# Cross attention's keys and values by Strassen's method, in a fused decoder and gated cross-attention kernel

## The chip, the cores and the metric

The kernel runs on one core of one Trainium2 chip, in float32 throughout. The metric is the device time of one execution in microseconds (us); less is better. A core has five engines with an instruction queue each: PE (matrix products), DVE, ACT and POOL (elementwise work), and SP, which here does nothing but issue DMAs. Each works through its own queue in order and waits at an instruction until what it needs is there.

## The reference

Sixteen sequences of 128 tokens with 512 channels and 16 heads of 32 go through a decoder layer (self-attention, cross-attention to `ctx_2048`, MLP) and then a gated cross-attention to the normalized `ctx_2048`. Cut to what matters here:

```python
ln_out = layernorm(hidden_states, ln1_s, ln1_b)
q, k, v = jnp.split(ln_out @ w_qkv + b_qkv, 3, axis=-1)
x = hidden_states + merge_heads(attention(q, k, v, ltor_mask)) @ w_ao + b_ao     # per head
ln_out = layernorm(x, ln2_s, ln2_b)
q = ln_out @ w_q + b_q
k, v = jnp.split(encoder_states @ w_kv + b_kv, 2, axis=-1)
x = x + merge_heads(attention(q, k, v, cross_mask)) @ w_co + b_co
x = x + gelu(layernorm(x, ln3_s, ln3_b) @ w1 + b1) @ w2 + b2
# then: x + tanh(gate) * gated cross attention of x to layernorm(encoder_states)
```

The change concerns the line with `w_kv`, the keys and values of cross-attention.

## The kernel before

**Groups, batches, units, steps.** The 16 sequences are four groups of four batches. A group's activations `x[g]` stay in SBUF from start to end (128 partitions, 4 batches, 512 channels). An attention stage is a list of sections, one for each group: A0 to A3 (self-attention), B0 to B3 (cross-attention), D0 to D3 (gated). `attend` goes through a section in 16 steps, four for each batch; a step handles one unit, four heads of one batch. In the step k of unit k, PE makes the scores (at each batch's first step), DVE scales them and POOL adds the mask; one step later DVE takes the minimum and ACT the exponentials (four activations); two steps later DVE takes the reciprocal of the sums and POOL normalizes; three steps later DVE transposes in 32x32 squares and SP sends the tile to device memory (`away`). The pair of units comes back as `pT` five steps later, PE mixes the values at step 10 counted from the batch's first (`mix`, product `av`), ACT copies the result (`mT`), and PE makes the output projection (`mo`) at step 12, which DVE adds to `x[g]`.

**Work beside the attention.** Beside section n stand the jobs of section n+1 (`jobs`: its queries, keys and values) and the preparations of section n+2 (`prepare`: normalizing `x[g]`, sending it to device memory and back so that channels lie on the partitions, loading the encoder's rows in blocks). So group 0's cross-attention projections run beside A3, and those of groups 1 to 3 beside B0, B1 and B2. Which job stands in which step is written out by hand: `plan` takes lists of jobs with lists of steps, and the order of the program is the order of every queue. `afterwards` defers an instruction to the start of the next step (`due`).

**Plain and Strassen projections.** A plain projection (`project_chunk`, `values_chunk`) makes 4 chunks of 4 matmuls with 512 columns. `block_product` makes the same as a product of 2x2 blocks by Strassen's method in Winograd's form: 7 products of 4 matmuls with 256 columns. `left_blocks` and `right_blocks` give the blocks and the four sums on either side. Products 1, 6 and 7 add up in one PSUM bank (`mm0`), which ACT copies out after each; 5 and 3 share `mm1`; 2 and 4 take `pt`, and DVE adds these in. Before the change self-attention and gated attention make queries, keys and values so; cross-attention makes all three plainly, with the value bias as a row (`bcv`) that DVE adds to the values. Tables such as `SECOND_BLOCKS` and `BLOCKS` say which product stands in which step:

```python
    SECOND_BLOCKS = (
        {4: (1, 2), 5: (6, 5), 6: (7, 4), 8: (3,)},
        {7: (1, 2), 8: (6,), 9: (7, 5), 10: (4,), 11: (3,)},
        {12: (1,), 13: (6, 2), 14: (7, 5), 15: (4, 3)},
    )
```

**Other work in these stages.** The weights of the gated stage are loaded as blocks, turned by DVE and written back to device memory (`gated_weight`): k and v beside self-attention, q beside B0 and o beside B1, with the loads in steps 0 to 7 and the turns in steps 8, 10, 12 and 14. Beside B2, `FirstGated.prepare` loads the turned k and v weights. Beside B3 run the first gated keys and values (`beside_last_cross`) and the first pieces of the MLP. Weight tiles rotate through six buffers (tag `w`), score tiles through eight (tag `s`), which the MLP and the last batch's transposes use too. Nearly all instructions are issued through a helper on line 49, so rows of the profile all name L49 and are told apart by their tiles: `mm_k_B` is the PSUM tile of cross-attention's keys, `mm_v_B` that of its values, `mo_B` and `mT_B` as above; `_A` is self-attention, `_D` gated attention, `h` and `o` the MLP.

Of the kernel before, what the change touches and what calls it, by code (L numbers as in the profile page):

```python
# [16 lines left out]
P = 128  # L17
NB = 16
S = 128
Q = 32  # L20
# [32 lines left out]
def decoder_then_gated_cross_attention(ctx: ExitStack, tc: tile.TileContext, a: dict, out: bass.AP):  # L53
# [24 lines left out]
    def afterwards(engine, do):  # L78
        late[engine].append(do)
# [32 lines left out]
    for b in range(GB):  # L112
# [8 lines left out]
            ("b_k", a["L0_xattn_b_kv"][0:H]), ("ln3_s", a["L0_xattn_ln3_s"]), ("ln3_b", a["L0_xattn_ln3_b"]),  # L121
# [199 lines left out]
    def values_chunk(v, wt, actT, b, name, bias_row=None):  # L321
# [4 lines left out]
        if bias_row is None:  # L326
            afterwards("act", lambda: nc.scalar.copy(v[:, b, :], mm))
        else:
            afterwards("dve", lambda: nc.vector.tensor_tensor(v[:, b, :], mm, bias_row, ALU.add))
# [151 lines left out]

    GATED_BLOCKS = (
# [54 lines left out]
    def scale_unit(bt, j):  # L537
        s = work.tile([P, NQ, KC, Q], F32, tag="s", name=f"s_{bt.name}_{j}", bufs=8)
        if bt.by_array:
            s = s.rearrange("p n c j -> p (n c j)").rearrange("p (c n j) -> p n c j", c=KC, n=NQ)  # L540
        bt.s[j] = s
        bt.sec.scale_mask(by_head(s), bt.sc.pop(j).rearrange("p (c n k) -> p c n k", c=KC, n=NQ), bt.b)
# [30 lines left out]
    def turn_by_array(bt, j):  # L573

        s = by_head(bt.s.pop(j)).rearrange("p c n k -> p c (n k)")
        tp = ps("sc", f"tp_{bt.name}_{j}")
        for c in range(KC):
            nc.tensor.transpose(tp[:, c * S : (c + 1) * S], s[:, c], ident)
        pT = work.tile([P, KC, NQ, Q], F32, tag="s", name=f"pT_{bt.name}_{j}", bufs=8)
# [263 lines left out]

    CROSS = {
# [15 lines left out]
    class CrossAttention(Section):  # L860
# [123 lines left out]
    def mlp(ml, last_steps):  # L984
# [8 lines left out]
        def sums_of(g, t):  # L993
            s3, s2, s4 = (quarter(work, "s", f"sx{n}_{g}", 8) for n in range(3))
# [103 lines left out]
        def projected_out(g, p, mm, acc):  # L1098
# [3 lines left out]
            if p == 0:  # L1102
                acc["m1"] = quarter(work, "s", f"m1_{g}", 8)
# [6 lines left out]
            elif p == 5:  # L1110
                acc["u2"] = quarter(work, "s", f"u2_{g}", 8)
                add(acc["u2"], mm, acc["m1"], ALU.add)
                gadd(x12, x12, acc["u2"], ALU.add)
            elif p == 6:
                acc["u3"] = quarter(work, "s", f"u3_{g}", 8)
# [3 lines left out]
            elif p == 4:  # L1119
                m5 = quarter(work, "s", f"m5_{g}", 8)  # L1120
# [97 lines left out]
    def fetch_part(key, t, n):  # L1218
        nc.sync.dma_start(out=t[:, n], in_=gated[key][:, n])
# [26 lines left out]

    class FirstGated:


        def prepare(self, p):  # L1250
# [5 lines left out]
            elif p < 3 * GB:  # L1256
                key, k = ("gk", "gv")[p // GB - 1], p % GB
# [246 lines left out]
    def beside_last_cross():  # L1504
        flip[0] = 2
        def piece():
# [6 lines left out]
            *gated_start(first), *mlp_start(ml), ([piece] * len(at_), at_),  # L1513
# [93 lines left out]
```

## Time and profile before

| | |
|---|---|
| Median of 3 runs | 1185.05 us (1183.89 to 1185.69) |
| The profiled execution | 1185.11 us, span 1183.2 us |
| PE busy | 1148.6 us (97%), 7010 records |
| DVE busy | 754.2 us (64%) |
| ACT busy | 592.6 us (50%) |
| POOL busy | 673.9 us (57%) |
| DMA | 253.70 MB, mean 214 GB/s |
| Mean granted PE clock | 0.992 |

The span is the time from the first to the last instruction; what lies around it is the difference to the execution's time. A busy share is an average over stages with different limits, so what bounds a stage is read from that stage alone. Every float32 matmul leaves two records in the trace, so counts of PE records are twice those of instructions. In rows of engines, the number after "x" is the count; "mean ns" is the mean duration of one; what stands in brackets with an arrow is what ended the idle time ahead of the instruction.

### The profile page before, as it was taken

The page shows a single profiled execution, that of the slowest core. Times are in us where ns is not written, and L with a number is a line of the kernel's source. Part 1 is how long each engine was busy: PE and PEld are TensorE (multiplying, and loading weights), DVE is VectorE, ACT ScalarE, POOL GpSimd, SP SyncE. Part 2 cuts the span into 40 slices and gives each one's busy share as a digit, 9 for nine tenths or more (in the row PEclk, how much of TensorE's full clock was granted, in tenths as well). Part 3 has the DMA queues.
Part 4 walks back from the last instruction along what each step waited for, and adds up shares of the span by engine and source line. Part 5 has one row for each costly group of instructions (what it writes and reads, how often), then busy time and mean ns, then how long its engine had stood idle before and what let it go on. Part 6 is the DMA issues. An engine that isn't in the chain of part 4 may idle for free.

```text
span 1183.2 us, 21051 instructions
## 1 busy us (share of the span) xinstructions
PE 1148.6 (97%) x7010; PEld 828.7 (70%) x7010; DVE 754.2 (64%) x1493; ACT 592.6 (50%) x2061; POOL 673.9 (57%) x612
## 2 busy tenths in 40 slices
PE   6999999999999999998999999999999989999998
PEld 5877777644444444445788888888888767778775
DVE  7677878776877767867644534442432268887773
ACT  2467767666655656655321223222222237876753
POOL 6698878675757656676233514433341356554873
PEclk9999999999999999998999999999999999999999
DMA  6588979898988978798796484596457728988874
GB/s 215 145 216 225 234 191 221 227 266 199 200 229 196 238 211 226 195 276 254 237 309 219 135 270 167 182 294 224 152 177 257 202 56 219 233 226 240 247 205 161
DMA packets 321796, 253.70 MB, mean 214 GB/s; under 512 B 83156, under 2 KB 279960, under 8 KB 316824
## 3 DMA queue, kind: packets, MB, share of 16 engines
q1 hardware_dynamic: 321648, 252.34, 75.5%
q8 instruction: 56, 0.92, 0.3%
q14 instruction: 52, 0.43, 0.1%
q10 hardware_dynamic: 40, 0.01, 0.0%
HBM read 161.06 MB, written 91.23 MB: 213 GB/s over the span
## 4 chain that ended last, share of the span: by engine, by line
PE 50%; DVE 1%; ACT 1%; issue 1%; POOL 1%; DMA 0%; SPq 0%; POOLq 0%; ACTq 0%
PE h L49 16%; PE o L49 16%; PE mm_q_D L49 4%; PE mm_v_D L49 3%; PE mm_k_D L49 3%; PE mm_o_D L49 3%; PE sc_D L49 1%; PE av_D L49 1%; PE mo_D L49 1%; PE mo_B L49 1%; POOL x L49 1%; ACT s_B L49 0%; DVE s_D L49 0%; DMA pT_D<-away_D 0%; ACT v_D L49 0%
## 5 line engine op out<-in xcount | busy, mean ns | idle before, releaser
L49 ACT ACTIVATE s_B<-s_B,mn_B 128x128 f32<-128x128 f32 x256 | 99.5, 391 | 74.3 <-issue 54.4
L49 DVE TENSOR_TENSOR h<-h,h 128x512 f32<-128x512 f32 x80 | 54.9, 686 | 117.3 <-PE h L49 117.0
L49 ACT ACTIVATE s_A<-s_A,mn_A 128x128 f32<-128x128 f32 x256 | 99.6, 394 | 53.7 <-issue 37.3
L49 ACT ACTIVATE h<-h 128x512 f32<-128x512 f32 x64 | 40.4, 631 | 160.4 <-DVE h L49 160.4
L49 ACT ACTIVATE s_D<-s_D,mn_D 128x128 f32<-128x128 f32 x256 | 99.5, 392 | 33.3 <-issue 12.1
L49 POOL TENSOR_TENSOR s_D<-s_D,sum_D 128x512 f32<-128x512 f32 x64 | 66.6, 1041 | 73.4 <-DVE sum_D L49 71.5
L49 POOL TENSOR_TENSOR s_B<-s_B,sum_B 128x512 f32<-128x512 f32 x64 | 67.5, 1054 | 60.6 <-DVE sum_B L49 48.7
L49 POOL TENSOR_TENSOR s_A<-s_A,sum_A 128x512 f32<-128x512 f32 x64 | 66.7, 1042 | 48.4 <-DVE sum_A L49 48.0
L49 POOL TENSOR_TENSOR s_A<-s_A,ma 128x512 f32<-128x512 f32 x64 | 81.4, 1271 | 5.5 <-DVE s_A L49 3.9
L49 POOL TENSOR_TENSOR s_B<-s_B,mask 128x512 f32<-128x512 f32 x64 | 81.5, 1273 | 4.3 <-DVE s_B L49 2.3
L49 POOL TENSOR_TENSOR rstd_aD<-rstd_aD,mhalf 128x1 f32<-128x1 f32 x12 | 6.6, 551 | 114.7 <-DVE rstd_aD L49 101.5
L49 POOL TENSOR_TENSOR sh<-h 128x512 f32<-128x512 f32 x32 | 40.7, 1273 | 50.4 <-ACT h L49 43.3
L49 PE MATMUL mo_B<-w_co,mT_B 128*128 128x512 f32 x128 | 61.6, 626 | 3.2 <-ACT mT_B L49 3.2
L49 PE MATMUL h<-T_C,w 128*128 128x256 f32 x256 | 61.0, 381 | 0.8 <-DVE h L49 0.8
L49 PE MATMUL h<-T_C,t 128*128 128x256 f32 x256 | 60.7, 380 | 0.1
L49 PE MATMUL h<-sx,t 128*128 128x256 f32 x256 | 60.6, 379 | 0.0
L49 PE MATMUL o<-t,h 128*128 128x256 f32 x256 | 60.5, 379 | 0.0
L49 PE MATMUL o<-t,sh 128*128 128x256 f32 x256 | 60.5, 379 | 0.0
L49 PE MATMUL o<-w,h 128*128 128x256 f32 x256 | 60.5, 379 | 0.0
L49 PE MATMUL mo_A<-w_ao,mT_A 128*128 128x512 f32 x128 | 59.1, 604 | 0.0
L49 PE MATMUL mm_v_B<-w_cv,T_e 128*128 128x512 f32 x128 | 57.7, 599 | 0.0
L49 PE MATMUL mm_q_B<-T_B,w_cq 128*128 128x512 f32 x128 | 57.3, 595 | 0.0
(297 smaller groups left out, 2904.7 us busy)
## 6 DMA issues: line engine op xcount, KB each, us to landing
t<-kept SPq DMA_DIRECT2D x24, 1024.0 KB
away_A<-s_A SPq DMA_DIRECT2D x64, 256.0 KB
pT_A<-away_A SPq DMA_DIRECT2D x128, 128.0 KB
away_B<-s_B SPq DMA_DIRECT2D x64, 256.0 KB
pT_B<-away_B SPq DMA_DIRECT2D x128, 128.0 KB
away_D<-s_D SPq DMA_DIRECT2D x60, 256.0 KB
pT_D<-away_D SPq DMA_DIRECT2D x120, 128.0 KB
w<-in_L_xattn_w_dram SPq DMA_DIRECT2D x24, 512.0 KB
```

The costliest lines, as they stand in the source:

```text
L49: return lambda *args, **kw: self.tc.keep_in_program_order(call(*args, **kw))
```

## The change

Keys and values of cross-attention are made by `block_product`, as self-attention's are; the query stays plain, in steps 1, 2, 3 and 5. Four weight sums for the keys are made once by DVE (`k_sum`, steps 4 and 5 beside A3), four for the values once by POOL (`v_sum`, steps 9 to 12). Four sums of encoder activations are made by POOL for each group, in steps 0 to 3 beside the section before. Three of them need room: they are written over batches 0 to 2 of that group's own `x[g]`. So `x[g]` is first written to device memory (`keep_part`, in steps 11 and 13 of the group's preparations), and is read back in steps 5, 9, 13 and 15 of the group's own section (6, 12, 17 and 19 for the last), before the residual is added to it. The weight sums take one tile `w`, one tile `row` and a new constant tile `sums_c`; score tiles go from eight buffers to seven. The value bias comes as a column (`b_cv`) in the activation that copies the mixed values, four activations of 128 columns in place of one copy of 512. The gated weights q and o load in steps 8 to 15, and are turned in steps 0, 2, 4 and 6 of the next section; `FirstGated` loads its weights four steps later.

```diff
-            ("b_k", a["L0_xattn_b_kv"][0:H]), ("ln3_s", a["L0_xattn_ln3_s"]), ("ln3_b", a["L0_xattn_ln3_b"]),
+            ("b_k", a["L0_xattn_b_kv"][0:H]), ("b_cv", a["L0_xattn_b_kv"][H : 2 * H]),
+            ("ln3_s", a["L0_xattn_ln3_s"]), ("ln3_b", a["L0_xattn_ln3_b"]),
...
+    CROSS_BLOCKS = (
+        {6: (1,), 7: (6, 2), 9: (7, 5), 10: (4,), 11: (3,)},
+        {11: (1,), 13: (6, 2), 14: (7, 5), 15: (4, 3)},
+    )
...
-        s = work.tile([P, NQ, KC, Q], F32, tag="s", name=f"s_{bt.name}_{j}", bufs=8)
+        s = work.tile([P, NQ, KC, Q], F32, tag="s", name=f"s_{bt.name}_{j}", bufs=7)
...
+    sums_c = cpool.tile([P, 2, HF], F32, tag="sums_c", name="sums_c")
...
-                elif g == 1:
-                    w["bcv"] = load_row(a["L0_xattn_b_kv"][H : 2 * H], "bcv_row")
...
+            if p in (11, 13):
+
+                for b in range(p - 11, p - 9):
+                    keep_part(f"x_{n}", x[g], b)
...
-            in_blocks[0] = False
...
-            out = [lambda c=c: project_chunk(self.q, w["cq"], lnT, c, f"q_{n}", "b_q", 0) for c in range(KC)]
-            out += [lambda c=c: project_chunk(self.k, w["ck"], encT, c, f"k_{n}", "b_k", 0) for c in range(KC)]
-            out += [lambda b=b: values_chunk(self.v, w["cv"], encT, b, f"v_{n}", w["bcv"]) for b in range(GB)]
+            tokens_at = [x[g][:, b].rearrange("p (o t) -> p o t", t=HF) for b in range(3)]
+            token_sides, sums = right_blocks(encT, tokens_at)
+            if g == 0:
+                self.begin()
+            products = [
+                block_product(halves(self.k), self.k_sides, token_sides, False, f"k_{n}", ("b_k", 0)),
+                block_product(by_quarters(self.v), self.v_sides, token_sides, True, f"v_{n}"),
+            ]
             return plan(
-                (out, PRODUCTS), ([lambda: mask_terms(self.ms, self.ma)], [7]),
-                *(gated_weight("qo"[g - 1]) if g in (1, 2) else ()),
-                *((late_weights(),) if g == 0 else ())
+                ([lambda c=c: self.query_chunk(c) for c in range(KC)], [1, 2, 3, 5]),
+                *blocks_plan(products, CROSS_BLOCKS), ([lambda: mask_terms(self.ms, self.ma)], [7]),
+                ([lambda o=o: nc.gpsimd.tensor_tensor(*o) for o in sums], [0, 1, 2, 3]),
+                *(self.weights_begin() if g == 0 else decoder[NG + g - 1].tokens_again([5, 9, 13, 15])),
+                *turned_beside(g),
+            )
+
+        def query_chunk(self, c):
+            project_chunk(self.q, w["cq"], self.lnT, c, f"q_{self.name}", "b_q", 0, ("mm0", "mm1")[c % 2])
+
+        v_bias = "b_cv", 0
+
+        def tokens_again(self, at_):
+            return [([lambda b=b: fetch_part(f"x_{self.name}", x[self.g], b) for b in range(GB)], at_)]
+
+        def begin(self):
+            t = wpool.tile([P, GB, 2, HF], F32, tag="w", name="sums_c")
+            row = work.tile([P, 2, HF], F32, tag="row", name="sums_c_row", bufs=2)
+            CrossAttention.sums_at = [t[:, n] for n in range(GB)] + [row, sums_c]
+            CrossAttention.k_sides, CrossAttention.v_sides = [], []
+
+        def weights_begin(self):
+
+            def sums(sides, key, n, engine):
+                new, todo = left_blocks(w[key], self.sums_at[n : n + 3])
+                sides.extend(new)
+                return [lambda o=o: engine.tensor_tensor(*o) for o in todo]
...
+            return (
+                late_weights(), ([lambda n=n: k_sum(n) for n in range(4)], [4, 4, 5, 5]),
+                ([lambda n=n: v_sum(n) for n in range(4)], [9, 10, 11, 12]),
             )
...
+    beside = {}
+
+    def turned_beside(g):
+
+
+        if g == 1:
+            beside["q"] = gated_weight("q", None, range(8, 16), [0, 2, 4, 6])
+            return beside["q"][:1]
+        if g == 2:
+            beside["o"] = gated_weight("o", None, range(8, 16), [0, 2, 4, 6])
+            return beside["q"][1], beside["o"][0]
+        return beside["o"][1:] if g == 3 else ()
...
-            elif p < 3 * GB:
-                key, k = ("gk", "gv")[p // GB - 1], p % GB
+            elif p >= 2 * GB:
+                key, k = ("gk", "gv")[p // GB - 2], p % GB
...
-            *gated_start(first), *mlp_start(ml), ([piece] * len(at_), at_),
+            *gated_start(first), *mlp_start(ml), *decoder[-1].tokens_again([6, 12, 17, 19]), ([piece] * len(at_), at_),
```

More of the change, by code (lines that the diff above doesn't have):

```diff
@@ L319, in project_chunk, with values_chunk @@
             afterwards("act", lambda: nc.scalar.activation(t[:, c, :], mm, AF.Identity, bias=col(bias, bias0 + c)))
-    def values_chunk(v, wt, actT, b, name, bias_row=None):
+    def values_chunk(v, wt, actT, b, name):
         mm = ps("mm", f"mm_{name}_{b}")
@@ L325, in values_chunk @@
             nc.tensor.matmul(mm, actT[:, k, b * S : (b + 1) * S], wt[:, k, :], start=(k == 0), stop=(k == KC - 1))
[L326 to L329, printed above, removed]
+        afterwards("act", lambda: nc.scalar.copy(v[:, b, :], mm))
     def qkv_tiles(sec):
@@ L578, in turn_by_array @@
             nc.tensor.transpose(tp[:, c * S : (c + 1) * S], s[:, c], ident)
-        pT = work.tile([P, KC, NQ, Q], F32, tag="s", name=f"pT_{bt.name}_{j}", bufs=8)
+        pT = work.tile([P, KC, NQ, Q], F32, tag="s", name=f"pT_{bt.name}_{j}", bufs=7)
         bt.pT[j] = pT.rearrange("p c n q -> p n c q")
@@ new lines, in weights_begin, with k_sum, v_sum @@
+        def weights_begin(self):
[3 more added lines that the diff above has]
+                return [lambda o=o: engine.tensor_tensor(*o) for o in todo]
+            todo = {}
+            def k_sum(n):
+                if n == 0:
+                    todo["k"] = sums(self.k_sides, "ck", 0, nc.vector)
+                todo["k"][n]()
+            def v_sum(n):
+                if n == 0:
+                    todo["v"] = sums(self.v_sides, "cv", 3, nc.gpsimd)
+                todo["v"][n]()
+            return (
+                late_weights(), ([lambda n=n: k_sum(n) for n in range(4)], [4, 4, 5, 5]),
+                ([lambda n=n: v_sum(n) for n in range(4)], [9, 10, 11, 12]),
@@ L993, in sums_of @@
         def sums_of(g, t):
-            s3, s2, s4 = (quarter(work, "s", f"sx{n}_{g}", 8) for n in range(3))
+            s3, s2, s4 = (quarter(work, "s", f"sx{n}_{g}", 7) for n in range(3))
             quarters = [[t[i][:, :, j * HF : (j + 1) * HF] for j in range(2)] for i in range(2)]
@@ L1102, in projected_out @@
             if p == 0:
-                acc["m1"] = quarter(work, "s", f"m1_{g}", 8)
+                acc["m1"] = quarter(work, "s", f"m1_{g}", 7)
                 add(acc["m1"], mm, half_row(ml.b2), ALU.add)
@@ L1110, in projected_out @@
             elif p == 5:
-                acc["u2"] = quarter(work, "s", f"u2_{g}", 8)
+                acc["u2"] = quarter(work, "s", f"u2_{g}", 7)
                 add(acc["u2"], mm, acc["m1"], ALU.add)
@@ L1114, in projected_out @@
             elif p == 6:
-                acc["u3"] = quarter(work, "s", f"u3_{g}", 8)
+                acc["u3"] = quarter(work, "s", f"u3_{g}", 7)
                 add(acc["u3"], mm, acc["u2"], ALU.add)
@@ L1119, in projected_out @@
             elif p == 4:
-                m5 = quarter(work, "s", f"m5_{g}", 8)
+                m5 = quarter(work, "s", f"m5_{g}", 7)
                 add(m5, mm, half_row(ml.db2), ALU.add)
@@ L1504, in beside_last_cross @@
     def beside_last_cross():
-        flip[0] = 2
+        flip[0], in_blocks[0] = 2, False
         def piece():
```

## The prediction

> **What bounds the kernel now.** I read the busy rows of the page first, then one table of stages whose borders are the starts of score matmuls, so that each row is four batches of attention with the next group's projections beside them. The columns are length, then busy time and records of PE, PEld, DVE, ACT and POOL, the granted clock, the DMA share and GB/s.
>
> ```profile
> PE   6999999999999999998999999999999989999998
> DVE  7677878776877767867644534442432268887773
> POOL 6698878675757656676233514433341356554873
> PEclk9999999999999999998999999999999999999999
> ```
> ```profile
> 118.94:180.07 61.13, 60.34 (x457) 44.44 (x456) 49.58 (x105) 42.15 (x169) 48.49 (x45) 1.00 0.83 212
> 226.58:291.55 64.97, 64.97 (x385) 30.84 (x385) 46.90 (x98) 41.15 (x162) 43.45 (x40) 1.00 0.94 239
> 291.55:356.52 64.97, 64.97 (x386) 30.84 (x385) 49.10 (x102) 39.66 (x154) 43.46 (x40) 1.00 0.88 211
> 356.52:421.49 64.97, 64.97 (x386) 30.84 (x385) 49.12 (x102) 40.74 (x151) 43.51 (x40) 1.00 0.90 215
> 421.49:486.46 64.97, 64.97 (x386) 30.84 (x385) 46.00 (x98) 38.47 (x150) 38.84 (x36) 1.00 0.82 219
> ```
>
> The last four rows are where cross attention's projections run (group 0's beside self-attention's last group, the others beside the cross group before them). All four are 64.97 us long and PE never rests in them: PE's own work sets this stage, and DVE, ACT and POOL have 16 us or more of idle time each. The first row is self-attention's third group, whose queries, keys and values are already by Strassen: 61.13 us, with 0.78 us of PE idle.
>
> The timeline of PE gives the prices:
>
> ```profile
> 94.38 1.89 PE L49 MATMUL mm_v_A<-w_sv,T_A 128*128 128x256 f32 x8
> 96.11 1.89 PE L49 MATMUL mm_v_A<-sums,T_A 128*128 128x256 f32 x8
> ...
> 328.68 7.03 PE L49 MATMUL mm_k_B<-T_e,w_ck 128*128 128x512 f32 x16
> 335.63 1.08 PE L49 MATMUL av_B<-pT_B,v_B 128*32 128x128 f32 x32
> ```
>
> A matmul shows as two records. A Strassen product (4 matmuls of 256 columns, 8 records) takes 1.73 us from start to start. Two plain chunks (16 records of 512 columns) take 6.95 us including the step to the next group of matmuls; between plain chunks it is 3.44 us each.
>
> **The change part by part.** (1) *PE.* Keys and values of four groups are eight projections. Each was 4 chunks, 4 x 3.44 = 13.76 us; it becomes 7 products, 7 x 1.73 = 12.09 us. Gain 1.67 us each, 8 x 1.67 = 13.4 us. From the other side: self-attention's row without its stall is 61.13 - 0.78 = 60.35 us with three Strassen projections; with the query left plain it would be 60.35 + 1.67 = 62.0 us, against 64.97, a gain of 2.95 us a group, 11.8 us in four. The difference of the two is what more and smaller groups of matmuls lose at scores and mixes. I take **11.8 us**, a measured row of the same structure, and keep 13.4 as the upper end.
>
> (2) *DVE.* Values needed four adds a group (691 ns) and still do. Keys now need four more: +2.8 us a group, 49.1 to about 51.9 of 62 us. Self-attention's row has 49.6 of 61 and holds its pace, so this should mostly lie beside PE. In the groups after the second, the turns of the gated q and o weights (4 x 0.69 us) move from steps 8 to 14 into steps 0, 2, 4 and 6, where the next group's normalizing already stands. DVE was busy 26.7 us in steps 0 to 7 of the row from 356.52; with the turns and one new add it has 30.1 us of work, and PE passes these steps in 32.5 - 1.7 = 30.8 us. What is late then is the exponential on ACT, and behind it the copy of the mixed values, for which the output projection on PE waits. Before, that copy ended 2.9 us ahead of PE's need (387.2 against 390.1 us); step 6 is now shorter on PE by 1.7 us and the copy longer by 0.9 us, which leaves about 0.3 us before any lateness of DVE. I charge 0.5 us in each of two groups, 1.0 us (0 to 3).
>
> (3) *ACT.* Keys: four activations of 670 ns become six of 470, no difference. Values: three copies of 585 ns. The value bias, now added to the mixed values, makes four activations of 360 ns out of one copy of 575 ns in each batch, +0.87 us. A group adds 5.4 us, to 46 of 62 us: hidden in the steady state, apart from the copy just named. At the end of the stage it is not:
>
> ```profile
> 541.60 6.34 PE L49 MATMUL mo_B<-w_co,mT_B 128*128 128x512 f32 x8 [3.15 <-ACT mT_B L49]
> ...
> 547.78 1.89 PE L49 MATMUL h<-T_C,w 128*128 128x256 f32 x8
> ```
>
> Here PE stood for 3.15 us on just this copy, and the bias makes it 0.87 us later: **+0.9 us**.
>
> (4) *POOL.* Four sums of activations a group at 1.27 us (self-attention's same sums), +5.1 us, to 48.6 of 62; self-attention's second group ran with 55.1 of 61. They are queued in steps 0 to 3, where POOL has 12.4 of 16.2 us of work, so the normalizing of scores behind them comes some 1.5 us late; their first reader is the second key product in step 7. Hidden. Values' four weight sums, once, in steps 9 to 12 of self-attention's last group, also: POOL has 10.7 and 9.2 of 16.2 us there.
>
> (5) *Keys' weight sums on DVE*, four in steps 4 and 5 beside self-attention's last group. The last quarter of that weight is loaded in step 3, so DVE can stand until it lands, with everything behind it: two score reductions, the scaling of scores, later the exponentials. After step 4 DVE usually waits 3 us for the output projection (2.96 us in the row from 356.52), which covers a part. Four sums with both operands in SBUF: such sums, of the MLP's weights, took DVE 0.66 us when POOL was idle and 1.35 to 1.53 us beside POOL. The Trainium skill, "SBUF — State Buffer", in its list on the shared port pair, speaks against putting them there: a VectorE instruction with two SBUF inputs and a GpSimd instruction exclude each other for their whole length. By the row at its best the sums cost 4 x 0.66 = 2.6 us of DVE, which those 3 us cover: a charge of 0, and the sum below would be 1.5 us better. By the rule they cost 4 x 1.4 = 5.6 us, 2.6 us beyond the cover, with POOL held up as well, and the sum would be 1.1 us worse. Between these, with the waiting for the load, I charge PE **1.5 us** (0 to 4), once.
>
> (6) *Transfers.* Each group's 1 MB of activations is written out and read back: 32 more DMAs of 256 KB, 8.4 MB on 253.7 MB. A group moved 211 GB/s x 65 us = 13.7 MB; now 15.8 MB in 62 us, 255 GB/s. The row from 226.58 held 239 GB/s over a group, and a quarter of it 273, without PE idle. SP issues 8 more at 0.43 us, 3.4 us a group; writes are queued in steps 11 and 13 of the group two ahead, reads in steps 5, 9, 13 and 15, each at least eight steps before the residual add that needs it. The gated q load waits at step 8 for self-attention's last output projection (its buffer), some 4 us in which a transposed score tile stands behind it on SP; that tile is wanted two steps later. One score buffer less (7 for 8) asks that a tile's transfer has left after three steps instead of four. All these I cost at nothing, covered by about two steps (7 us); at the tail two reads of 256 KB fall into a stretch at full DMA share, 0.5 us (0 to 2).
>
> Sum: 11.8 - 1.0 - 0.9 - 1.5 - 0.5 = 7.9 us. The profiled execution took 1185.11 us around its span of 1183.2, practically the median of 1185.05, so the forecast is 1185.1 - 7.9 = **1177.2 us**.
>
> **The rivals.** *All of it hidden*: 13.4 us less the 0.9 of the tail, 1172.6 us. For it: self-attention's rows. Against it: DVE's 30.1 of 30.8 us in steps 0 to 7.
>
> *PE stands long enough for its clock to fall* (the one on the other side). Where PE waited 3.15 us for ACT, the clock went to 0.50 and eight records took 6.34 us instead of 3.53:
>
> ```profile
> 541.00:547.00 6.00, 5.40 (x7) 2.30 (x8) 2.21 (x6) 2.20 (x10) 5.92 (x6) 0.50 1.02 311
> 547.00:549.00 2.00, 2.00 (x9) 1.39 (x8) 1.55 (x3) 1.39 (x7) 1.92 (x2) 1.00 0.87 250
> ```
>
> Waits of 1.07 us and less (self-attention) cost only themselves. The Trainium skill, "TensorE: Matmul & The Clock Gate", part 1, says that a window of about 3.4 us of idleness halves the clock until a busy window has passed; by it the 3.15 us would not always be enough, here it was. If the mixed-value copy comes 3 us late at step 8, each such wait costs 3.15 + 2.8 = 6 us; one in every group is 24 us against 11.8, 1197 us. It decides from two such waits on: 12 us eat the gain. Against it: a late PE lets DVE and ACT catch up, and no wait in self-attention's three rows of this structure passes 1.1 us.
>
> *Transfers bind*: if the stage gave no more than its usual 239 GB/s, 15.8 MB need 66 us a group and nothing is gained: 1184 to 1188 us. For it: DMA shares about 0.9. Against it: 273 GB/s were seen, and 311 at the tail.
>
> *It is not what it says*: the counts of instructions in the built program fit (PE +96 matmuls, DVE +20, POOL +20, ACT +68, SP +32); left out.
>
> **How the numbers follow.** Main case, most of the gain kept, 0.62; all hidden 0.16; transfers bind 0.10; clock falls 0.12. 0.2% is 2.4 us, about what a measurement can tell from no change: faster means below 1182.7. Main (4 to 11 us of gain) and all-hidden are faster nearly whole, and a little of the transfer case: 0.80. Same 0.07, slower 0.13. The range runs from the upper end of the PE gain with no charge but the tail, 1172, to 1184, where the transfer case begins.
>
> **What would show it.** Right: rows of about 62 us for four batches in the four stages, PE idle under 1.5 us in each, keys' and values' products at 1.73 us, the tail wait for the mixed copy near 4 us at half clock, MLP and gated stages unchanged in length. The first of the four rows should be the longest. Wrong: PE waiting for ACT's mixed copy in every batch or longer than 3 us, rows of 65 us, a clock under 1.00 inside the stage, or POOL's sums still running when the second key product is due.

## The result, and the profile after

| | before | changed |
|---|---|---|
| Median of 14 runs, first occasion | 1183.38 us (1181.78 to 1185.69) | 1186.47 us (1180.18 to 1192.03) |
| Ratio, first occasion | | 1.0017 (1.0003 to 1.0031) |
| Ratio, second occasion (kernel "again" below) | | 0.9985 (0.9976 to 0.9993) |
| The profiled execution | 1185.11 us, span 1183.2 us | 1182.92 us, span 1181.0 us |

The one occasion says a little slower, the other a little faster; both lie within 0.2% of no change. The forecast was 7.9 us faster. The same kernel differs by 0.3% between the two occasions, so ratios of different occasions are not compared more closely than that. The changed kernel's own runs spread over 12 us, and the slowest have the lowest granted clock: the fastest run, 1180.18 us, has a mean of 0.995, the slowest, 1192.03 us, 0.988 (though 1188.30 us stands at 0.994). By an estimate from these two means, 0.007 of 1180 us, some 8 of the 12 us are clock; which waits of PE lower it is not shown. The profiled execution, at 1182.92 us, is 3.6 us under the median, so the profile shows the loss of one of the faster runs.

The same table of stages for the changed kernel (four batches a row, columns as before):

```profile
224.39:287.24 62.85, 61.72 (x433) 39.96 (x433) 54.10 (x106) 42.09 (x167) 54.17 (x49) 1.00 0.96 259
287.24:348.97 61.73, 61.72 (x434) 39.96 (x433) 49.12 (x102) 41.61 (x164) 47.87 (x45) 1.00 0.86 215
348.97:412.84 63.87, 62.17 (x434) 40.01 (x433) 51.26 (x106) 41.65 (x166) 48.21 (x45) 1.00 1.00 250
412.84:475.24 62.40, 61.71 (x433) 39.96 (x433) 47.34 (x99) 40.02 (x153) 41.06 (x38) 1.00 0.96 264
```

They sum to 250.85 us, against 4 x 64.97 = 259.88: **9.0 us were gained** where the change was made. (The first row starts 2.2 us earlier than before; the kernels below that are alike up to there start it at 224.39 to 226.78, so no gain is read from that.) The next stage, the last cross section beside the first gated keys and values and the first MLP pieces, gave it back. Its first three batches, before and then changed:

```profile
486.46:502.70 16.24, 16.24 (x97) 7.71 (x96) 15.19 (x38) 9.77 (x37) 10.66 (x12) 1.00 0.73 198
502.70:515.51 12.81, 12.81 (x89) 6.19 (x89) 9.12 (x19) 7.98 (x35) 8.54 (x8) 1.00 1.02 269
515.51:528.32 12.81, 12.81 (x89) 6.19 (x89) 8.38 (x17) 7.59 (x34) 10.85 (x11) 1.00 0.99 274
```
```profile
475.24:492.31 17.07, 16.31 (x97) 7.71 (x96) 15.30 (x37) 11.62 (x47) 10.52 (x11) 1.00 0.78 228
492.31:506.83 14.52, 13.28 (x89) 6.32 (x88) 12.69 (x28) 12.36 (x53) 11.62 (x12) 1.00 0.90 264
506.83:521.29 14.46, 13.21 (x90) 6.35 (x89) 7.56 (x16) 6.94 (x33) 9.32 (x9) 1.00 1.00 271
```

Before, PE never rested in these three batches, but there was little to spare: transfers were full in two of them (share 1.02 and 0.99), and DVE was busy 15.2 of 16.2 us in the first. Changed, each is longer, by 4.2 us in all, and what follows, up to the MLP matmul `h` that waits 0.79 us for DVE, by 3.0 us more (37.4 and 40.4). From the section's first scores to that `h` it was 79.25 us (486.46 to 565.71) and is 86.48 (475.24 to 561.72), **7.2 us back**. The timeline of PE names the waits (their time stands in the brackets; the view of the first line ends inside its group):

```profile
477.18 3.27 PE L49 MATMUL mo_B<-w_co,mT_B 128*128 128x512 f32 x7 [0.76 <-ACT mT_B L49]
493.94 3.70 PE L49 MATMUL mo_B<-w_co,mT_B 128*128 128x512 f32 x8 [0.46 <-ACT mT_B L49]
502.21 1.07 PE L49 MATMUL av_B<-pT_B,v_B 128*32 128x128 f32 x28 [0.79 <-DMA pT_B<-away_B]
516.66 1.07 PE L49 MATMUL av_B<-pT_B,v_B 128*32 128x128 f32 x28 [1.25 <-DMA pT_B<-away_B]
531.62 1.07 PE L49 MATMUL av_B<-pT_B,v_B 128*32 128x128 f32 x28 [1.75 <-DMA pT_B<-away_B]
534.94 5.40 PE L49 MATMUL mo_B<-w_co,mT_B 128*128 128x512 f32 x8 [2.26 <-ACT mT_B L49]
546.94 1.07 PE L49 MATMUL av_B<-pT_B,v_B 128*32 128x128 f32 x28 [2.80 <-DMA pT_B<-away_B]
```

With two short waits for DVE in MLP matmuls, 0.39 and 0.79 us, they add to 11.3 us, against 4.4 us before (0.48, 3.15 and 0.79). `pT_B` is the transposed score pair that comes back from device memory. It is late either because transfers are slow, or because the tile was sent late. Both are so, as two more views show. ACT's waits in the stage before it (total, times, longest), first of the kernel before and then of the changed one:

```profile
ACT T_a L49 <- DMA back_a<-turned_D: 0.3, 1, 0.3
```
```profile
ACT T_a L49 <- DMA back_a<-turned_D: 3.5, 1, 3.5
```

and DVE's timeline around the section's start, in the same order (first scores at 486.46 and at 475.24):

```profile
483.16 0.14 DVE L49 RECIPROCAL sum_B<-sum_B 128x4 f32<-128x4 f32 x1
483.78 2.01 DVE L49 TENSOR_TENSOR db<-vcols 128x2 f32<-128x2 f32 x4
486.57 0.69 DVE L49 TENSOR_TENSOR v_B<-mm_v_B,bcv_row 128x512 f32<-128x512 f32 x1 [0.77 <-PE mm_v_B L49]
```
```profile
476.14 0.18 DVE L49 RECIPROCAL sum_B<-sum_B 128x4 f32<-128x4 f32 x1 [4.08 <-ACT s_B L49]
476.81 2.01 DVE L49 TENSOR_TENSOR db<-vcols 128x2 f32<-128x2 f32 x4
478.75 0.67 DVE L49 TENSOR_TENSOR v_B<-v_B,mm_v_B 128x512 f32<-128x512 f32 x1
479.34 0.68 DVE L49 TENSOR_TENSOR v_B<-mm_v_B,v_B 128x512 f32<-128x512 f32 x1
```

ACT, which works in order, stands 3.5 us at the activation of `T_a` (the gated stage's inputs, by way of device memory). Behind it are the exponentials, for which DVE stands 4.1 us. DVE passes the same instruction (`db`) 2.7 us ahead of the section's first scores before the change, and 1.6 us after them now.

### The profile page after: what moved, and what is told of

Its sections match the earlier page's. It is cut to its first block, busy times and chain, and to the rows that moved or that the text cites. A ratio compares the mean times of both kernels' runs of the same rounds, so it can differ in the third digit from the quotient of the medians.

```text
span 1181.0 us, 21615 instructions
## 1 busy us (share of the span) xinstructions
PE 1136.5 (96%) x7202; PEld 865.3 (73%) x7202; DVE 766.9 (65%) x1513; ACT 605.3 (51%) x2129; POOL 697.2 (59%) x632
## 4 chain that ended last, share of the span: by engine, by line
PE 45%; DMA 3%; issue 2%; POOL 2%; DVE 2%; ACT 1%; SPq 1%; POOLq 0%; DVEq 0%; ACTq 0%
PE o L49 16%; PE h L49 16%; PE mm_q_D L49 4%; PE mm_k_D L49 3%; PE mm_v_D L49 2%; PE mo_D L49 1%; PE mm_o_D L49 1%; DMA away_D<-s_D 1%; PE sc_D L49 1%; SPq L49 1%; PE av_D L49 1%; POOL s_D L49 1%; PE mo_B L49 1%; POOL x L49 1%; DVE s_D L49 0%
## 5 line engine op out<-in xcount | busy, mean ns | idle before, releaser
L49 ACT ACTIVATE s_D<-s_D,mn_D 128x128 f32<-128x128 f32 x256 | 99.4, 391 | 33.3 <-issue 14.5
L49 PEld LDWEIGHTS h<-T_C,w 128*128 128x128 f32 x256 | 48.2, 190 | 8.9 <-DVE h L49 1.9
```

Of the source, the lines that this page charges most:

```text
L49: return lambda *args, **kw: self.tc.keep_in_program_order(call(*args, **kw))
```

## The experiments

In the table, "rows" is the sum of the four stages, "section" the stretch from the last cross section's first scores to that `h`, "T_a" ACT's wait for `back_a`; each from one profile (in "again" and before_round_trip the profile names something else as what ended that wait). Ratios are of all runs, with 95% intervals, to the kernel before on the same chip.

| kernel | ratio | rows | section | T_a |
|---|---|---|---|---|
| before | 1 | 259.88 | 79.25 | 0.3 |
| changed | 1.0017 (1.0003, 1.0031) | 250.85 | 86.48 | 3.5 |
| again | 0.9985 (0.9976, 0.9993) | 250.68 | 87.77 | 4.6 |
| no_tail_reads | 0.9967 (0.9955, 0.9978) | 249.48 | 81.84 | 2.8 |
| three_parts | 0.9958 (0.9945, 0.9970) | 248.83 | 84.50 | 3.1 |
| before_round_trip | 1.0022 (1.0013, 1.0032) | 260.41 | 82.12 | 1.0 |
| before_7_score | 1.0005 (0.9993, 1.0016) | 259.88 | 79.29 | 0 |
| three_parts_no_bias | 0.9980 (0.9971, 0.9989) | 249.71 | 89.31 | 4.3 |
| three_parts_early | 0.9957 (0.9945, 0.9969) | 250.20 | 83.98 | 3.4 |
| plain_last_group | 0.9928 (0.9912, 0.9945) | 253.56 | 77.57 | 1.9 |
| changed_gv_late | 0.9978 (0.9966, 0.9989) | 249.92 | 84.24 | 1.7 |
| three_parts_gv_late | 0.9955 (0.9938, 0.9972) | 248.72 | 82.81 | 1.3 |
| plain_last_gv_late | 0.9933 (0.9921, 0.9944) | 252.88 | 77.22 | 1.0 |
| before_loads_late | 1.0008 (1.0001, 1.0015) | 259.88 | 79.75 | 1.8 |
| gv_late_no_tail_reads | 0.9943 (0.9929, 0.9957) | 250.29 | 82.01 | 1.5 |
| plain_last_o_later | 0.9933 (0.9918, 0.9947) | 251.90 | 78.91 | 2.9 |
| changed_sums_early | 0.9968 (0.9957, 0.9978) | 250.49 | 86.19 | 4.1 |
| all_three_out | 0.9934 (0.9919, 0.9948) | 250.56 | 79.54 | 1.0 |
| three_parts_all | 0.9959 (0.9945, 0.9972) | 250.03 | 83.15 | 2.0 |
| plain_last_all | 0.9927 (0.9914, 0.9939) | 252.06 | 78.67 | 2.9 |

### Bytes in the last section

**again**, the changed kernel unedited:

> The changed kernel once more, for a second profile. Its first profile, an execution of 1182.9 us, is 3.6 us under the kernel's median. Theory 1 (transfers bind the last cross-attention section, so its stalls hang on how transfers happen to fall): the four batches between the score matmuls of the first group's self-attention end and the last cross section again take about 250 to 252 us (259.9 before), the last cross section again loses 6 to 11 us, and what differs between the two executions lies in that section, with lower granted clock there. Theory 2 (the stage itself swings): the four rows differ by more than 2 us between the profiles. Time 1182 to 1190 us.

Measured: the rows repeat within 0.2 us each, the section within 1.3 us. The loss is in the section each time.

**no_tail_reads:**

```diff
-            *gated_start(first), *mlp_start(ml), *decoder[-1].tokens_again([6, 12, 17, 19]), ([piece] * len(at_), at_),
+            *gated_start(first), *mlp_start(ml), ([piece] * len(at_), at_),
```

> The last group's activations are not read back (four reads of 256 KB in the last cross section left out, so that group's residual is not the right one); all else as changed. Theory 1 (transfers bind in the last cross section, 1 MB at about 265 GB/s is 3.9 us, and with it waits long enough to halve the clock): 4 to 7 us faster than the changed kernel of the same call, about 1180 us, and waits of PE for pT_B there under 0.5 us. Theory 2 (one score buffer less makes every transfer's lateness visible): no change from the changed kernel, waits stay. Theory 3 (the copy of the mixed values with bias is what is late): no change.

The section falls from 86.5 and 87.8 to 81.8 us. Of the single edits of the changed kernel this one saves the most, 4.6 us or more, but 2.6 us over before are left.

**three_parts:**

```diff
-                for b in range(p - 11, p - 9):
+                for b in range(p - 11, min(p - 9, 3)):
...
-            return [([lambda b=b: fetch_part(f"x_{self.name}", x[self.g], b) for b in range(GB)], at_)]
+            return [([lambda b=b: fetch_part(f"x_{self.name}", x[self.g], b) for b in range(GB - 1)], at_)]
```

> Only batches 0 to 2 of a group are overwritten by sums, so only these are sent away and read back: 24 DMAs of 256 KB in place of 32, one read less in the last cross section. Theory 1: a quarter of the extra transfers, about 1 us in the last section and perhaps 0.5 in the four stages, 1 to 2 us faster than the changed kernel. Theory 2 or 3: no change.

A fourth of the round trip was superfluous, as batch 3 is never overwritten. Leaving it out gains somewhat more than expected: 0.9958 against 0.9985 on the same chip.

**before_round_trip**, the reverse: the 32 DMAs added to the kernel before (`keep_part` in steps 11 and 13, `tokens_again` as in the changed kernel).

> The kernel before, with the changed kernel's 32 DMAs of activations alone, at the same steps (each group is written out and read back unchanged; nothing is made by Strassen's method in addition). Theory 1 (the extra bytes bind only where transfers are full): the four stages stay at 64.97 us a row, the last cross section grows by 3 to 6 us, 1186 to 1190 us. Theory 2 (buffers): 1183 to 1184 us, no change. If transfers bound the stages as well: rows above 65 us, 1190 us or more.

As theory 1 expects: three rows stay at 64.97 us and one grows by 0.5, while the section grows from 79.25 to 82.12 us. The 24 DMAs that lie in the four rows cost 0.5 us; the four reads here cost 2.9 us.

**before_7_score:**

```diff
-        s = work.tile([P, NQ, KC, Q], F32, tag="s", name=f"s_{bt.name}_{j}", bufs=8)
+        s = work.tile([P, NQ, KC, Q], F32, tag="s", name=f"s_{bt.name}_{j}", bufs=7)
```

> The kernel before with seven score buffers instead of eight, nothing else. Theory 1 (bytes in the last cross section): no change, within 1 us of before, rows 64.97. Theory 2 (the lost buffer is what lets late transfers reach PE): the last cross section 2 us longer or more, with PE waiting for pT_B in several batches, 1185 to 1188 us.

Rows and section are unchanged. The lost score buffer costs nothing in the kernel before. Eight buffers were not tried in the changed kernel, but all_three_out below reaches 79.54 us with seven, so theory 2 is not needed.

**three_parts_no_bias:**

```diff
-        v_bias = "b_cv", 0
+        v_bias = None
```

> Three parts sent away and read back, and the value bias left out (the mixed values are copied in one instruction, as before the change; the output then lacks that bias). Theory 3 (the longer copy costs at the last section's output projections): the waits of mo_B for mT_B of 0.3 to 0.5 us in the first batches go, the wait at the end falls from 3.7 to about 3 us, 1 to 2 us faster than with three parts alone. Theory 1: those waits are 1 us at most in sum, under 1 us faster, and the waits for pT_B stay.

The copy does shrink (0.57 us in place of 1.12), yet PE waits longer for it:

```profile
476.15 3.70 PE L49 MATMUL mo_B<-w_co,mT_B 128*128 128x512 f32 x8 [1.02 <-ACT mT_B L49]
```

In this execution ACT stood 4.3 us for `back_a`, and everything behind came later. So the copy's own length is not what made `mT_B` late; theory 3 falls as a main cause. Why this kernel is slower than three_parts (0.9958), and than three_parts_early on the same chip (0.9957, intervals apart), although it does less, is not shown: one profile shows the longer wait, but not why it should be longer in most runs.

**three_parts_early:**

```diff
-tokens_again([6, 12, 17])
+tokens_again([2, 1, 4])
```

> Three parts, and the last group's three reads moved from steps 6, 12 and 17 of the last cross section to steps 2, 1 and 4, its first batch, in which transfers were busy 0.73 to 0.78 of the time and not 1.0. Theory 1: most of what the reads cost is saved, 1 to 3 us faster than three parts (about 1177 us), the waits for pT_B under 0.5 us each. If a backlog from the stage before is carried through the section anyway: no gain, the waits stay at 0.8 to 1 us.

A miss: 83.98 us where three_parts has 84.50. Placing the reads in the slack of the first batch saves almost nothing. DVE had entered 1.5 us after the first scores here as well, which points to something carried in from the stage before.

**plain_last_group:**

```diff
             qkv_tiles(self)
+            if g == NG - 1:
+                return self.plain_jobs()
```

(`plain_jobs` has the plain chunks of the kernel before at its steps, and loads again the two weight quarters that sums had overwritten.)

> Three parts, and the last group's keys and values plain again (the quarters of the two weights that sums overwrote are loaded again, four DMAs of 128 KB), so that this group is not sent away. Theory 1: its row (beside the group before) goes back to about 65 us, +2.6, and the last cross section loses its three reads and the backlog of its writes: to within 1.5 us of before, -5 against the changed kernel; in sum 1 to 3 us faster than three parts. Theory 2 or 3: only the 2.6 us are lost and nothing is gained, 1181 to 1182 us.

The fastest kind here. Its fourth row is 64.97 us, and its batches in the section run at 16.25, 12.81 and 12.80 us. That the section takes 77.6 us, less than before, lies in what follows them: 35.7 us in place of 37.4, where the last output projections ran at 3.70 us in place of 6.34. Giving up one group's gain of 2.6 us saves 7 to 9 us behind it.

### What is carried in

**changed_gv_late:** the loads of `w_gv`, which the change had moved from steps 8 to 11 to steps 12 to 15, right beside `back_a`, go behind it.

```diff
-            elif p >= 2 * GB:
-                key, k = ("gk", "gv")[p // GB - 2], p % GB
...
+            elif 2 * GB <= p < 3 * GB:
+                self.load("gk", p % GB)
...
+            ([lambda k=k: first.load("gv", k) for k in range(KC)], range(KC)),
             *gated_start(first), *mlp_start(ml),
```

> The changed kernel with one edit: the four loads of the gated value weight (256 KB each) move from steps 12 to 15 beside the third cross section to steps 0 to 3 of the last one (first used in its step 7). Theory 4 (in steps 12 to 15 they delay back_a, for which ACT waits 3.5 us ahead of the exponentials; DVE then waits 4.1 us, enters the last section 4 us late against PE, is nearly full there and cannot catch up): ACT's wait for back_a falls under 1.5 us, DVE's db sums end before the section's first scores, the last section loses 2 to 4 us less, 1179 to 1181 us where the changed kernel has 1182 to 1186. Theory 1 alone (only the sum of bytes counts): the bytes stay, they move into the section that is full; no gain or 1 us slower.

ACT's wait halves (1.7 us), `db` now starts 0.2 us ahead of the first scores, the first batch is back at 16.24 us, and the section takes 84.24 us, 2.2 less than changed, although 1 MB of loads moved into it. The ratio, 0.9978, is not apart from 0.9985, though.

**three_parts_gv_late** and **plain_last_gv_late**, the same edit on two others:

> The same edit on the kernel with three parts sent away. Theory 4: 2 to 4 us faster than three parts (0.996 of before), 1175 to 1177 us, batches of the last section near 16.3, 13.2, 13.2 us. Theory 1 alone: 0.996 of before again.

> The same edit on the kernel whose last group is made plainly. Its last section already ran at 16.25, 12.81 and 12.80 us a batch with a 1.9 us wait of ACT for back_a, so that both theories expect little: 0 to 1 us, 1175 to 1176 us.

Sections 1.7 and 0.4 us shorter; the first one's time, 0.9955, is no better than 0.9958. The second is level, as expected.

**before_loads_late:**

```diff
-            elif p < 3 * GB:
-                key, k = ("gk", "gv")[p // GB - 1], p % GB
+            elif p >= 2 * GB:
+                key, k = ("gk", "gv")[p // GB - 2], p % GB
```

> The kernel before with the change's later loads alone: the gated key and value weights in steps 8 to 15 beside the third cross section instead of 4 to 11. Theory 4: ACT's wait for back_a grows from 0.3 us to 2 to 3 us; before, PE is 2.6 us slower over that section, so part of it is caught up: 0 to 2 us slower, a longer wait of mo_B at the end of the last section. Theory 1 alone: no change, 1184 us.

The loads alone raise the wait from 0.3 to 1.8 us. At the slower row DVE catches up (the section's fifth reciprocal starts 16.9 us after the first scores in both kernels), and 0.5 us is lost. So the moved loads cost 0.5 us behind the slower row, and about 2 us behind the shorter one. The row itself can be read off too: at nearly the same wait of ACT (1.8 us here, 1.7 us in changed_gv_late) `db` starts 2.1 us ahead of the first scores here and 0.2 us ahead there, 1.9 us less lead after a row that is 2.6 us shorter (64.97 and 62.40). The two kernels differ in more than that row, so this is a sign and no proof.

**gv_late_no_tail_reads:** both edits.

> The changed kernel with both edits of the last section: the gated value loads in its steps 0 to 3, and the four reads of the last group's activations left out (its residual is then not the right one). If bytes (reads) and the late entry (ACT waiting for back_a) are the two causes and add up: from the section's first scores to the MLP matmul that waits for DVE 79 to 80.5 us, as before the change (79.3; changed 86.5 and 87.8, without reads 81.8, with late loads 84.2), and 11 us less than before in all up to the gated stage, 1173 to 1175 us. If a third cause is left: 81.5 us or more there, 1177 us.

82.01 us, not 79 to 80.5: the two don't add up, and a third cause is left. With the reads out, moving the loads gains nothing (81.84 without it). The same reciprocal starts 19.0 us after the first scores, 2.1 later than before. In the first batch DVE has 15.3 us of work in 16.2 and hardly catches up. `db` stands 2.3 us later against the scores than before the change, and behind it come the two `v_B` adds of the values' last products, of the fence above; before the change one such add (0.69 us) stood there.

**plain_last_o_later:**

```diff
-        if g == 2:
-            return beside["q"][1], beside["o"][0]
-        return beside["o"][1:] if g == 3 else ()
+        if g == 2:
+            return beside["q"][1:]
+        return gated_weight("o", None, range(8), [8, 10, 12, 14]) if g == 3 else ()
```

> The plain-last kernel with late gated value loads, and the gated output weight loaded and turned beside the third cross section (loads in steps 0 to 7, turns in 8 to 14) in place of beside the second (8 to 15) and third (0 to 6). If it is its small transfers that delay back_B, for which ACT stands, and with it the copy of v_B: the second section's row falls from 63.3 to about 61.8 us; the third, made plainly, has 2.6 us more of PE's time and should stay at 65.0. 1 to 1.5 us faster than without (0.993 of before). If the third section's own transfers are too full then: its row above 65.5, or the last section above 78 us, and nothing is gained.

The row of the second cross section falls from 63.34 to 61.73 us, as expected if the gated output weight's small loads had delayed `back_B` (ACT stood 6.0 us for it in the changed kernel). That is not shown, though: three_parts and three_parts_gv_late have 61.73 us there with the loads in their old place. ACT now stands 2.9 us for `back_a`, beside which the turned weight's writes have come to lie, the section grows by 1.7 us, and nothing is gained.

**changed_sums_early:** DVE's `db` sums (2.0 us) leave the full batch.

```diff
-                *turned_beside(g),
+                *turned_beside(g), *((([bias_sums], [8]),) if g == NG - 1 else ()),
```

> The changed kernel with one edit: the four small DVE sums of the MLP's biases (db, 2.0 us), which stand at the start of the last cross section, move to step 8 of the section before, where DVE has 15 us of idle time. If it is DVE's late entry into a first batch in which it is busy 15.2 of 16.2 us that keeps the whole section behind: 1.5 to 3 us less in that section, from its first scores to the MLP matmul that waits for DVE 84 to 85 us (changed 86.5 and 87.8), about 2 us faster than the changed kernel. If only bytes count: no change.

0.9968, lower than either measurement of the changed kernel, but from another occasion, and its interval touches that of 0.9985. The second batch runs at 12.81 us, where it had 14.5. The section of the profiled execution took 86.19 us all the same, for there ACT stood 4.1 us and the third batch still waited for transfers; the expected length was missed.

**all_three_out:** no reads, late loads, early sums.

> The changed kernel without its four reads in the last section (that group's residual is then not the right one), with the gated value loads in its steps 0 to 3, and with the bias sums a section earlier. If bytes, ACT's wait for back_a and DVE's entry are all of it, the section is back to what it was before: 78 to 80 us from its first scores to the MLP matmul that waits for DVE (before 79.3, without the third edit 82.0), batches of 16.24, 12.8 to 13.0 us, about 9 us faster than before in all, 1174 us. If 82 us stay, DVE's entry is not the third cause.

Three batches and the rest of the section, from the windows of this kernel:

```profile
476.84:493.04 16.20, 16.20 (x97) 7.71 (x96) 15.15 (x38) 12.22 (x48) 11.59 (x13) 1.00 0.93 245
493.04:505.84 12.80, 12.80 (x89) 6.19 (x88) 9.12 (x19) 8.49 (x37) 8.54 (x8) 1.00 1.04 294
505.84:518.64 12.80, 12.80 (x89) 6.19 (x88) 8.21 (x16) 7.93 (x38) 10.35 (x10) 1.00 1.01 270
```

PE is full again, and the section is 79.54 us: what the prediction had wanted, once all three are out. The transfers are just as full as before (1.04 and 1.01); they are met because DVE is in time (the reciprocal at 17.0 us). The ratio, 0.9934, is not apart from the 0.9943 of two edits; the third cause rests on the profiles.

**three_parts_all** and **plain_last_all**, with nothing left out:

> Three parts sent away, gated value loads in the last section's steps 0 to 3, bias sums a section earlier: nothing left out, all four groups by Strassen's method. By the sum of causes 80 to 81 us in that section (three reads left, 2 to 3 us), 8 us faster than before in all, 1175 us. If the entry is no cause: 82.8 us there, 1178 us.

> The last group plain, gated value loads late, gated output weight beside the third section, and the bias sums a section earlier. The last section had 78.9 us with DVE entering 2 us later than in its sister (77.2): with the sums moved about 77.5, 1 to 1.5 us faster than that, 1174 to 1175 us. If the entry is no cause: 1175.9 us again.

The first is a miss: 83.15 us and no faster than three_parts. Its first two batches are full, and the third loses what the reads take:

```profile
490.61:503.41 12.80, 12.80 (x89) 6.19 (x88) 9.69 (x21) 9.05 (x41) 9.10 (x9) 1.00 1.02 292
503.41:516.21 12.80, 11.55 (x86) 5.88 (x86) 7.45 (x14) 6.47 (x31) 8.89 (x9) 1.00 1.05 277
```

Over all 20 profiles two of the causes can be told apart by batch. The second batch is full (12.81 us) in the ten whose fifth reciprocal (counted behind the one just ahead of `db` in the fences above) starts at most 17.6 us after the first scores, and 0.7 to 3.5 us longer in nine of the ten where it starts at 18.8 us or later (the tenth, changed_sums_early, lost its time in the first batch, 17.64 us). So that batch hangs on DVE's entry. Where the second is full, the third is too, at 12.80 or 12.81 us, except in the three such kernels that still have reads: 13.12 us (before_round_trip), 14.39 (changed_sums_early) and 14.46 (three_parts_all).

plain_last_all measured 1175.17 us (1174.27 to 1177.14), 0.7% faster than before. It is not apart from the three other plain-last kernels.

## Why the prediction was wrong

The numbers in brackets are those of the prediction's terms.

(1) *PE*: right. Where nothing waits, a row is 61.73 us, 3.24 less than 64.97; the prediction had 2.95 to 3.35 for each.

(2) and (5) *DVE*: 2.5 us were charged inside the stages, which left 9.3 us of the gain; measured 9.0. Part of the agreement is luck: PE won 13.0 us (4 x 3.24) and waits took 3.9. The first row, with the weight sums, is 1.1 us over the second, where 1.5 were charged; the third is 2.1 over it and the fourth 0.7. The third swings: in kernels that are alike up to there it is 61.73 us (three_parts) and 63.22 (three_parts_early). PE's waits in the rows are of one kind:

```profile
251.82 0.81 ACT L49 ACTIVATE k_B<-mm_k_B,vcols 128x256 f32<-128x256 f32 x2
252.74 1.97 PE L49 MATMUL mm_k_B<-x,sums_c 128*128 128x256 f32 x8 [1.13 <-issue]
...
401.46 0.81 ACT L49 ACTIVATE T_B<-back_B,vcols 128x512 f32<-128x512 f32 x1 [5.99 <-DMA back_B<-turned_B]
403.72 0.56 ACT L49 COPY v_B<-mm_v_B 128x512 f32<-128x512 f32 x1
404.34 1.99 PE L49 MATMUL mm_v_B<-sums_c,T_e 128*128 128x256 f32 x8 [1.69 <-ACT v_B L49]
...
440.74 1.97 PE L49 MATMUL mm_k_B<-x,sums_c 128*128 128x256 f32 x8 [0.69 <-POOL s_B L49]
```

Products 1, 6 and 7 share a PSUM bank, and by the program the next of them waits until ACT has copied out the one before. In the first row PE starts 0.1 us after the end of that copy (252.63), in the third 0.06 us after it (404.28). So exponentials that come late do reach PE, as the prediction had it, but by way of this copy, not of the mixed values' copy. In the third row ACT had stood 6.0 us for `back_B`, and not behind the turns of the q and o weights on DVE, which the charge of 1.0 us was for. The weight sums themselves:

```profile
239.70 1.51 DVE L49 TENSOR_TENSOR sums_c<-w_ck 128x512 f32<-128x512 f32 x1
241.25 1.64 DVE L49 TENSOR_TENSOR w_ck<-w_ck 128x512 f32<-128x512 f32 x1
...
246.38 1.25 DVE L49 TENSOR_TENSOR sums_c<-w_ck 128x512 f32<-128x512 f32 x1
247.67 0.69 DVE L49 TENSOR_TENSOR sums_c<-w_ck,sums_c 128x512 f32<-128x512 f32 x1
...
249.19 1.04 POOL L49 TENSOR_TENSOR s_A<-s_A,sum_A 128x512 f32<-128x512 f32 x1 [2.10 <-DMA T_e<-in_ctx_dram]
```

5.1 us together, near the 5.6 by the rule of the Trainium skill ("SBUF — State Buffer", its list on the shared port pair) and far from 2.6. The one at 0.69 us fell into the 2.1 us in which POOL was idle. (The profile puts that wait down to a transfer, but the instruction reads `sum_A`, whose reciprocal DVE started at 248.91, behind the sums.)

(3) *The bias at the tail*, +0.9 us: not seen, and too high by the reading. The four activations overlap: they take 1.1 us together, against 0.57 for the one copy, so 0.55 us more and not 0.87. The wait for the mixed copy at the stage's end was 2.26 us in the changed kernel and near 4 in three_parts, but longest of all without the bias, in three_parts_no_bias:

```profile
532.96 6.32 PE L49 MATMUL mo_B<-w_co,mT_B 128*128 128x512 f32 x8 [3.69 <-ACT mT_B L49]
```
```profile
537.33 5.96 PE L49 MATMUL mo_B<-w_co,mT_B 128*128 128x512 f32 x8 [4.50 <-ACT mT_B L49]
```

So other things set it, and what the bias adds to it can't be read off.

(4) *POOL*: hidden. The profile puts PE's wait of 0.69 us in the fourth row down to POOL, but that matmul does not read `s_B`; it is the second of the key products again, and started 0.15 us after ACT's copy of the first one ended (440.59).

(6) *Transfers*: **the step that failed.** "At the tail two reads of 256 KB fall into a stretch at full DMA share, 0.5 us" was the whole price of the section where the gain was lost; it cost 7.2 to 8.5 us. Three things are wrong in it. Four reads lie there, not two, in a stretch whose share of about 1.0 stood in the profile of before: 2.9 us alone (before_round_trip), 4.6 us and more as the change left it. The loads of the gated weights, moved by four steps to beside `back_a`, were not costed at all: about 2 us of section with the reads in it, nothing to be seen without them. And "covered by about two steps" took DVE's and ACT's lead over PE for granted. Part of it seems to come from the slower row: with a row 2.6 us shorter, and like waits of ACT, `db` had 1.9 us less lead (before_loads_late). The section's first batch, at 15.2 of 16.2 us on DVE, has no room to win it back.

How the 7.2 us divide stays open: reads, moved loads and DVE's entry overlap (leaving out two gave 82.0 us, all three 79.5), single profiles of one kernel differ by 1.3 us, and the clock at the section's end swings by 3.0 us (3.70 to 6.68 for the same eight records). What the median run lost beyond the profiled one is not shown either.

*The rivals.* "Transfers bind", at 0.10, came nearest in time (1184 to 1188), but at the wrong place: no row went back to 65 us. "Clock falls" did not decide in the profiles: after the wait of 2.26 us the output projections took 5.40 us, less than the 6.34 before the change. What share it has in the spread of the times is not shown by any profile.

## What to carry to other kernels

A gain on the bound engine ends where the next stage begins: price the stage behind it too, with its transfers and engines as full as its own rows show, and with the lead of the others shortened by a part of what was won (1.9 of 2.6 us in the pair above). List every DMA that a change moves, and look at what in-order engine waits for the transfer next to it. Here it paid to leave the last unit as it was, and so to spare the full stage behind it the traffic.

## What was not expected of the hardware

- A wait inside a group of matmuls costs more than the idle time shown ahead of it. In no_tail_reads `av_B` shows 0.42 us of waiting, while from its first matmul (499.16) to the next group's (501.00) it took 1.84 us in place of 1.01: 0.83 us. The excess of 0.4 us does not grow with the wait: in the changed kernel waits of 0.79, 1.25 and 2.80 us cost 1.18, 1.65 and 3.20. Prices are better taken from start to start.
- The length of the wait alone does not say whether PE's clock falls. After 2.31 us the same eight records ran at full speed in plain_last_group and took 6.12 us in again; after 2.26 us (changed) they took 5.40. In again and changed another wait, of 1.90 and 1.75 us, ended 3.3 to 3.4 us ahead of these records, in plain_last_group none did; but in plain_last_gv_late 2.46 us were enough (5.40) without such a neighbour, so what decides stays open. The two lines, plain_last_group first:

```profile
531.84 3.70 PE L49 MATMUL mo_B<-w_co,mT_B 128*128 128x512 f32 x8 [2.31 <-ACT mT_B L49]
```
```profile
537.31 6.12 PE L49 MATMUL mo_B<-w_co,mT_B 128*128 128x512 f32 x8 [2.31 <-ACT mT_B L49]
```
